# Two causal key tiles scored together, a bias add moved to VectorE, and new weights for the planner of a two-layer gated attention kernel

## The chip, the core and the metric

The kernel runs on one core of one Trainium2 chip. The core has TensorE (PE, matrix products), VectorE (DVE), ScalarE (ACT), GpSimd (POOL) and SyncE (SP, which here only issues transfers); each takes its instructions in order, and semaphores let one wait for another. The metric is the device time of one execution in microseconds. Before the change it is 2710.31 us, the median of three runs (2707.89 to 2714.53).

## What is computed

Eight sequences of 512 tokens and 256 channels pass through two layers. In each layer a gated cross attention and a gated feed-forward part are added to x. Cut to what matters here, with layer 0's attention in full:

```python
# layer 0, attention: 16 heads of 16 channels
q, k, v = heads(x @ Wq + bq), heads(x @ Wk + bk), heads(x @ Wv + bv)
att = q @ k.T * scale
att = where(causal, att, -inf)            # lower triangle of 512 x 512
y = softmax(att) @ v
qc, kc, vc = heads(x @ Wcq + bcq), heads(ctx @ Wck + bck), heads(ctx @ Wcv + bcv)
y = y + softmax(qc @ kc.T * scale) @ vc   # all 512 context rows
xattn = y @ Wp + bp
...
x = x + tanh(g_xattn[0]) * xattn(layernorm(x))
x = x + tanh(g_ffn[0]) * ffn0(layernorm(x))      # 8-bit quantized, gelu
x = x + tanh(g_xattn[1]) * block1(layernorm(x))  # two attention blocks (16 heads of 32), each with an MLP
x = x + tanh(g_ffn[1]) * ffn1(layernorm(x))      # ternary weights, depthwise convolution
```

Everything is float32 except the two feed-forward products, which are bfloat16 after quantization.

## The kernel before

The program is straight-line code that a Python program writes. It has four stages in time: attention of layer 0 (`layer0_xattn`), the first half of layer 0's feed-forward (`layer0_ffn`), then everything else woven together (`layer1_xattn`), with a tail for the last sequence. Between stages x and the hidden values are kept in DRAM.

**Attention of layer 0.** A sequence b is cut into two halves u of the heads, each into two groups e of four heads, and each group has two sides s: s = 0 is causal self attention, s = 1 is attention to the context. A side has four key tiles kt of 128 keys. `steps0` makes the list of steps. `front(e, s, kt)` (L1517) writes four products S = K·Q, one head on each of four 32-row strips of the array, into two PSUM tiles `ps_s` of two banks each; for the causal side only the queries from `lo = 128*kt` on are computed, so tiles 0 to 3 have 512, 384, 256 and 128 columns. Two ACT instructions (L1526) take the exponential from PSUM to `pt`, and for the causal side a GpSimd `affine_select` (L1529) sets the upper triangle of the 128x128 diagonal block of all four heads to zero in place. `back` (L1536) then multiplies with the values, one head on each of four 32-column strips of the array, and accumulates the four key tiles in one PSUM bank `ov` (the value tile holds ones beside the values, so that the sums come with it). After the last key tile DVE transposes `ov` (L1551), takes the reciprocal and scales.

The list holds front, back, front, back, ..., but `end_rest` (L1215) runs the back of the front before: on PE the order is front 1, back 0, front 2, back 1. `ps_s` has three buffers, of which a front takes two; `pt` has two; `ov` has one.

**The other streams.** Around those steps the Python program weaves what else is to be done: `norm0` (layer norm of the next sequence, and L1406, which adds the gated projection bias `gbp` to x once), `pre0` and `values0` (transposes and values), `pairs0` (Q and K of a group), `cross0`, `ctx0`, `post0` (projection and residual), `few_bits` (quantization of weights), `load1`.

**Who sets the order.** `weave_timed` (L1160) and, for the last stage, `weave_all` write one instruction group after another. Each stream has a place on a scale, its base plus its share times the part of it already written; the candidate with the lowest place is written next, among those whose inputs will be there within `soon` of the time at which PE comes free by a table of estimated costs (`Pace`). The numbers that set shares and bases are in `SET`, `FIRST_AT` and `LAST_AT` (L29 to L66, which hold a few others too). `FIRST_AT` and `LAST_AT` place the second half of layer 0's feed-forward (`first`) and layer 1's feed-forward (`last`) of each sequence between the sixteen attention slots of layer 1, in each of which one block of one sequence goes through 4 groups of 4 key tiles. A manual dependency keeps the instructions of every engine in the written order, so the numbers decide what stands behind what on each engine.

In layer 1, `ov` has a single buffer too: after the last key tile of a group the sums come from products with ones ("ps<-acc,ones" and "ps<-pt,ones"), then DVE makes `oT` in four instructions (L2362 to L2367), and only then may the next group's first back write `ov`.

Of the kernel before, what the change touches and what calls it, by code (L numbers as in the profile page):

```python
# [10 lines left out]
AF = mybir.ActivationFunctionType  # L11
ALU = mybir.AluOpType
# [3 lines left out]
P = 128  # L16
B, T, C, CC = 8, 512, 256, 128
H = 16
NT = T // P
# [6 lines left out]
MAGIC = 12582912.0  # L26
NEG = -1.0e30
ROWS = ((0, 1), (2, 3, 4), (5, 6, 7))
FIRST_AT = (-1.51, 0, 1, 2, 4, 3.86, 6.93, 9)  # L29
LAST_AT = (6.01, 6.53, 7.45, 11.96, 12.03, 13, 15)  # L30
PTS = 3
SET = dict(
    pairs0=0.758,
    post0=0.88,
    values0=1.2,
    few0=0.88,
    load1=0.88,
    norm0=0.88,
    ctx0=0.88,
    next0=0.847,  # L40
    gains=0.886,
    range_total=5.807,
    range_share=1.0,
    soon=0.336,
    change0=0.0,
    change1=0,
    first=1.046,
    first_lag=2.213,
    last=0.8,
    last_total=10.064,  # L50
    last_lag=1.534,
    mlp0=0.47,
    mlp1=0.597,
    mlp0_at=1.0,
    mlp1_at=1.0,
    pre=0.65,
    pre_at=-1.433,
    pre_lag=1.558,
    pair=0.2,
    pair_at=-0.25,  # L60
    keys=1.0,
    keys_at=-1.001,
    back=1.05,
    tail_at=17.0,
    half_at=0.0,
# [973 lines left out]
class Fast(General):  # L1039
# [348 lines left out]
    def norm0(self, b):  # L1388
        nc, work, x = self.nc, self.work, self.xs[b]
        if b:  # L1390
            self.load_ctx0(b)
        if 0 < b < B - 1:
            self.load_x0(b + 1)
        q = self.seqs[b]
        z = q["z"] = work.tile([P, NT, C], F32, tag="z", name="z", bufs=1)
        q["recs"] = work.tile([P, 8, 16], F32, tag="recs", name="recs")
        yield need(x, pe=False)
        yield from self.ln_timed(x, z, "n")
        if not b:
# [6 lines left out]
        nc.gpsimd.tensor_tensor(x, x, self.gbp.unsqueeze(1).to_broadcast([P, NT, C]), ALU.add)  # L1406

    def out_of(self, out, ps, scale, bias):

# [93 lines left out]
    def steps0(self, b, u):  # L1503

        nc, work, pace = self.nc, self.work, self.pace
        q = self.seqs[b]
        st = {}

        def front_at(e, s):
            if (u, s) not in q:
                return 1e9
            QT, KT = q[u, s]
            return max(pace.when([Pace.name(QT), Pace.name(KT[e])]), pace.place("st", 2))

        def front(e, s, kt):  # L1517
            QT, KT = q[u, s]
            lo = kt * P if s == 0 else 0
            pss = [self.st.tile([P, 2, T], F32, tag="st", name="ps_s") for _ in range(2)][::-1]  # L1520
            for j in (2, 3, 0, 1):
                r = slice(32 * j, 32 * j + 32)
                self.mm(pss[j // 2][:, j % 2, lo:], KT[e][r, kt * P : (kt + 1) * P], QT[r, lo:])
            pt = work.tile([P, 4, T], F32, tag="pt", name="pt", bufs=2)
            for jp in (1, 0):
                nc.scalar.activation(pt[:, 2 * jp : 2 * jp + 2, lo:], pss[jp][:, :, lo:], AF.Exp)  # L1526
            if s == 0:
                diag = pt[:, :, kt * P : (kt + 1) * P]
                nc.gpsimd.affine_select(  # L1529
                    out=diag, in_=diag, compare_op=ALU.is_ge, fill=0.0,  # L1530
                    base=0, pattern=[[0, 4], [1, P]], channel_multiplier=-1,
                )
            reads = [Pace.name(pt), Pace.name(self.vts[s][b % 2])]
            self.coming = (reads, kt == 0, lambda: back(e, s, kt, lo, pt), lambda: ("v", s) in q)

        def back(e, s, kt, lo, pt):  # L1536
            g = 2 * u + e
            if kt == 0:
# [3 lines left out]
            for j in (2, 3, 0, 1):  # L1542
                self.mm(
                    ov[32 * j : 32 * j + 32, lo:], vt[:, kt, 4 * g + j, :], pt[:, j, lo:],
                    kt == 0, kt == NT - 1,
                )
            if kt < NT - 1:
                return

            ot = work.tile([P, 16, 32], F32, tag="ot", name="ot", bufs=2)  # L1550
            nc.vector.transpose(ot.rearrange("p b d -> p (b d)"), ov)  # L1551
            rec = q["recs"][:, 4 * u + 2 * e + s, :]
            nc.vector.reciprocal(rec, ot[:, :, 16])
            recb = rec.unsqueeze(2).to_broadcast([P, 16, 16])
            if e == 0 and s == 0:
                st["yn"] = work.tile([P, 16, 32], F32, tag="yn", name="yn", bufs=2)
            yn = st["yn"][:, :, 16 * e : 16 * e + 16]
            if s == 0:
                nc.vector.tensor_tensor(yn, ot[:, :, 0:16], recb, ALU.mult)
                return  # L1560
            yc = work.tile([P, 16, 16], F32, tag="yc", name="yc", bufs=2)
            nc.vector.tensor_tensor(yc, ot[:, :, 0:16], recb, ALU.mult)
            nc.vector.tensor_tensor(yn, yn, yc, ALU.add)
            if e == 1:
                yT = self.out0.tile([P, T], F32, tag="yT", name="yT", bufs=3)
                nc.vector.transpose(yT, st["yn"].rearrange("p b d -> p (b d)"))
                q["yT", u] = yT
                if u == 1:
                    self.seen(q["recs"])

        def rest_at():
# [290 lines left out]
    def layer1_xattn(self):  # L1862
        nc, tc = self.nc, self.tc
        with (
# [838 lines left out]
```

## Time and profile before

The profiled execution took 2705.0 us, of which 2703.2 us lie between its first and its last instruction. The stages below are stretches of that span.

| stretch, us | what | PE busy | DVE busy | ACT busy | POOL busy | PE clock |
|---|---|---|---|---|---|---|
| 15 to 100 | layer 0 attention, sequence 0 | 75.6 of 85 | 29.0 | 45.5 | 16.2 | 1.00 |
| 185 to 270 | the same, one sequence later on | 83.4 of 85 | 41.4 | 59.7 | 16.6 | 1.00 |
| 725 to 848 | layer 0 feed-forward, first half | 89.3 of 123 | 95.3 | 81.1 | 1.7 | 0.86 |
| 860 to 2500 | layer 1, woven | 1528.8 of 1640 | 1145.3 | 847.9 | 457.9 | 0.97 |
| 2500 to 2600 | layer 1, last sequences | 84.6 of 100 | 70.8 | 43.3 | 9.4 | 0.95 |
| 2600 to 2704 | tail | 58.0 of 104 | 73.8 | 23.9 | 2.5 | 0.77 |

How to read it: "busy" is the time in which an engine had an instruction at work. For PE an end is modelled, and a product that waits inside its group can be counted as busy, so 98% is not yet PE at its peak. The clock is the share of full speed that the throttle granted to PE in the stretch.

Of the costs that the change touches, the trace has these rows: the exponential takes 1022, 809, 597 and 380 ns for 1024, 768, 512 and 256 elements (L1526), the `affine_select` of L1529 646 ns in the mean (128 of them), and L1406 2362 ns on GpSimd (eight of them).

### The profile page before, as it was taken

The numbers are of one execution on the slowest core, as the hardware profiler recorded it, in microseconds if no ns is written. First come the engines' busy times: TensorE is split into PE (matmuls) and PEld (weight loads), VectorE is DVE, ScalarE is ACT, GpSimd is POOL, SyncE is SP. The second block draws the span as 40 slices with busy tenths as digits, with TensorE's granted clock in tenths as the row PEclk, the third lists the DMA queues.
The fourth block names the chain that finished last, engine by engine and source line by source line (L and its number), as shares of the span: only waits on it lengthen the run. The fifth ranks groups of instructions, "written<-read, shape, count | busy, mean of one in ns | idle before, by whom it ended". The sixth has DMA issues, their size and how long they took to land.

```text
span 2703.2 us, 67872 instructions
## 1 busy us (share of the span) xinstructions
PE 2443.5 (90%) x30128; PEld 1012.8 (37%) x30128; DVE 1711.0 (63%) x3116; ACT 1470.0 (54%) x1831; POOL 614.6 (23%) x682
## 2 busy tenths in 40 slices
PE   6999999999776989999999899999899999999865
PEld 2333333333233334434534433434344444343343
DVE  4444554344377666664576677768856677877767
ACT  4667776666573545544455454455454454655431
POOL 2212222111101444330254221102123431201100
PEclk9999999999987999999999899999999999999987
DMA  3011120100265412210221012021030101201000
GB/s 113 8 48 52 52 74 7 32 33 13 94 281 195 169 48 95 76 63 29 98 69 38 19 45 85 34 87 64 17 122 22 42 28 60 75 29 40 25 25 18
DMA packets 74431, 170.58 MB, mean 63 GB/s; under 512 B 7184, under 2 KB 36240, under 8 KB 66832
## 3 DMA queue, kind: packets, MB, share of 16 engines
q1 hardware_dynamic: 71744, 162.94, 17.2%
q8 instruction: 238, 3.90, 0.6%
q0 software_dynamic: 800, 2.62, 0.3%
q10 hardware_dynamic: 1584, 0.58, 0.1%
q14 instruction: 65, 0.53, 0.1%
HBM read 103.21 MB, written 62.91 MB: 61 GB/s over the span
## 4 chain that ended last, share of the span: by engine, by line


## 5 line engine op out<-in xcount | busy, mean ns | idle before, releaser
L2318 ACT ACTIVATE pt<-ps_s 128x1024 f32<-128x1024 f32 x512 | 496.4, 1021 | 397.0 <-PE ps_s L1146 274.0
L1146 PE MATMUL ps_s<-QT,KT 32*128 32x512 f32 (+3 forms) x4096 | 620.5, 607 | 21.3 <-ACT pt L2318 13.6
L1526 ACT ACTIVATE pt<-ps_s 128x1024 f32<-128x1024 f32 (+3 forms) x512 | 412.2, 862 | 176.9 <-PE ps_s L1146 167.0
L1146 PEld LDWEIGHTS ps_s<-QT,KT 32*128 32x128 f32 x4096 | 194.5, 184 | 381.4 <-issue 189.4
L1146 PE MATMUL ov<-pt,vt 128*32 128x512 f32 (+3 forms) x1792 | 202.0, 521 | 53.2 <-DVE oT L2367 28.5
L1142 PE MATMUL ps<-x3T,li 128*32 128x256 f32 x4096 | 242.1, 389 | 0.1
L1146 PE MATMUL ov<-pt,v 128*32 128x512 f32 (+3 forms) x2048 | 231.1, 521 | 10.5 <-POOL pt L1529 10.5
L1142 PE MATMUL ps<-li,hD 128*32 128x256 f32 x4096 | 231.4, 380 | 5.5 <-ACT hD L2265 5.5
L2322 POOL TENSOR_SCALAR_AFFINE_SELECT dg<-pt 128x512 f32<-128x512 f32 x128 | 121.5, 949 | 477.9 <-ACT pt L2318 477.9
L2078 POOL TENSOR_SCALAR mv<-mv 128x2 f32<-128x2 f32 (+1 forms) x105 | 46.9, 446 | 603.2 <-DVE mv L2073 578.3
L1529 POOL TENSOR_SCALAR_AFFINE_SELECT pt<-pt 128x512 f32<-128x512 f32 x128 | 82.7, 646 | 438.5 <-ACT pt L1526 434.8
L1142 PEld LDWEIGHTS ps<-li,hD 128*32 128x32 f32 x4096 | 133.0, 110 | 98.4 <-issue 11.1
L1142 PEld LDWEIGHTS ps<-x3T,li 128*32 128x32 f32 x4096 | 131.0, 113 | 103.3 <-issue 24.0
L2349 DVE TENSOR_TENSOR acc<-acc,pt 128x2048 f32<-128x2048 f32 x64 | 153.0, 2390 | 2.2 <-ACT pt L2318 0.9
L2347 DVE TENSOR_TENSOR acc<-pt 128x2048 f32<-128x2048 f32 x64 | 151.7, 2370 | 0.0
L2433 DVE SCALAR_TENSOR_TENSOR hF<-hp,cols,hF 128x256 f32<-128x256 f32 x224 | 112.8, 503 | 42.2 <-ACT hF L2424 36.2
L1142 PE MATMUL ps<-zT,a_wq 128*32 128x512 f32 x1024 | 123.5, 602 | 3.6 <-DVE zT L2159 2.3
L1551 DVE STREAM_TRANSPOSE ot<-ov 128x512 f32<-128x512 f32 x64 | 45.8, 715 | 127.8 <-PE ov L1146 127.5
L1142 PE MATMUL ps<-li,oT 128*32 128x256 f32 x2048 | 122.7, 380 | 2.4 <-DVE oT L2367 1.2
L1854 ACT ACTIVATE hD<-ps,cols 128x256 f32<-128x256 f32 x119 | 53.2, 473 | 119.7 <-PE ps L1142 76.7
L1856 DVE TENSOR_SCALAR hD<-ps,cols 128x256 f32<-128x256 f32 x137 | 62.7, 480 | 68.3 <-PE ps L1142 48.1
L2424 ACT ACTIVATE hF<-hp,cols 128x256 f32<-128x256 f32 x54 | 32.4, 600 | 131.8 <-DVE hp L2421 131.8
(304 smaller groups left out, 3578.2 us busy)
## 6 DMA issues: line engine op xcount, KB each, us to landing
hd<-h SPq DMA_DIRECT2D x16, 1024.0 KB, 3.9
hF<-hd SPq DMA_DIRECT2D x16, 1024.0 KB, 6.5
li<-in_w_a_dram SPq DMA_DIRECT2D x12, 1024.0 KB, 5.3
xF<-xd SPq DMA_DIRECT2D x22, 512.0 KB, 5.0
kd<-k SPq DMA_DIRECT2D x8, 1024.0 KB, 5.2
vd<-v SPq DMA_DIRECT2D x8, 1024.0 KB, 5.4
res<-rd SPq DMA_DIRECT2D x32, 256.0 KB, 2.7
vt<-vd SPq DMA_DIRECT2D x8, 1024.0 KB, 5.2
```

Source lines behind the costliest of these rows:

```text
L1142: self.nc.tensor.matmul(out[j : j + 32], lhsT[:, j : j + 32], rhs, start=start, stop=stop, skip_group_check=True)
L1146: self.nc.tensor.matmul(out, lhsT, rhs, start=start, stop=stop, skip_group_check=True)
L1526: nc.scalar.activation(pt[:, 2 * jp : 2 * jp + 2, lo:], pss[jp][:, :, lo:], AF.Exp)
L1529: nc.gpsimd.affine_select(out=diag, in_=diag, compare_op=ALU.is_ge, fill=0.0, base=0, pattern=[[0, 4], [1, P]], channel_multiplier=-1,)
L1854: self.nc.scalar.activation(out, ps, AF.Identity, bias=bias)
L1856: self.nc.vector.tensor_scalar(out, ps, bias, None, ALU.add)
L2078: nc.gpsimd.tensor_scalar(rstd, mv[:, :, 1], EPS, None, ALU.add)
L2318: nc.scalar.activation(pt[:, 2 * jp : 2 * jp + 2, :], pss[jp], AF.Exp)
L2322: nc.gpsimd.affine_select(out=dg, in_=pt[:, :, diag], compare_op=ALU.is_gt, fill=0.0, base=0, pattern=[[0, 4], [-1, P]], channel_multiplier=1,
L2347: nc.vector.tensor_tensor(st["acc"], st["pt"], pt, ALU.add)
L2349: nc.vector.tensor_tensor(st["acc"], st["acc"], pt, ALU.add)
L2433: nc.vector.scalar_tensor_tensor(a, hp[:, half + k : half + k + n], self.col("conv_w", 3 * f + k), a, ALU.mult, ALU.add)
```

## The change

Three edits. (1) `front` and `back` take a list of key tiles. On the causal side the four steps (0), (1), (2), (3) become three, (0), (1, 3), (2): the 128 columns of tile 3 and the 384 of tile 1 stand side by side in the same two `ps_s` tiles (tile 3 at columns 0 to 127, tile 1 behind), one pair of exponentials takes all 512, and one `affine_select` takes both diagonal blocks, which stand at columns 0 to 255. The back multiplies tile 1, then tile 3, into `ov`; key tile 2 is now the last. The context side keeps its four steps. (2) L1406 is issued on VectorE instead of GpSimd. (3) Some 25 numbers of the planner are set anew, which rewrites the order of all stages.

The number of PE products and the columns that they run over stay as they were. Counted in the two written programs, layer 0's attention has 255 runs of row-strip products before and 223 after; 256 and 224 runs of column-strip products; 26 and 26 of whole-array transposes. In layer 1 the same counts are 256 and 256, 282 and 286, 86 and 85.

```diff
-FIRST_AT = (-1.51, 0, 1, 2, 4, 3.86, 6.93, 9)
-LAST_AT = (6.01, 6.53, 7.45, 11.96, 12.03, 13, 15)
+FIRST_AT = (-1.51, -0.4, 1, 2, 4, 3.86, 7.6, 9)
+LAST_AT = (6.01, 6.53, 8.78, 11.96, 12.49, 13, 16.76)
 SET = dict(
-    pairs0=0.758,
-    post0=0.88,
-    values0=1.2,
+    pairs0=1.659,
+    post0=0.932,
+    values0=0.0,
...
-    norm0=0.88,
-    ctx0=0.88,
-    next0=0.847,
-    gains=0.886,
+    norm0=0.541,
+    ctx0=1.787,
+    next0=0.959,
+    gains=1.202,
...
-    soon=0.336,
+    soon=0.475,
...
-    pre=0.65,
+    pre=1.019,
...
-    pair_at=-0.25,
-    keys=1.0,
-    keys_at=-1.001,
+    pair_at=-0.48,
+    keys=0.91,
+    keys_at=-0.936,
...
-        nc.gpsimd.tensor_tensor(x, x, self.gbp.unsqueeze(1).to_broadcast([P, NT, C]), ALU.add)
+        nc.vector.tensor_tensor(x, x, self.gbp.unsqueeze(1).to_broadcast([P, NT, C]), ALU.add)
...
-        def front(e, s, kt):
+        def front(e, s, kts):
             QT, KT = q[u, s]
-            lo = kt * P if s == 0 else 0
+            at, parts = 0, []
+            for kt in kts[::-1]:
+                lo = kt * P if s == 0 else 0
+                parts.insert(0, (kt, lo, slice(at, at + T - lo)))
+                at += T - lo
             pss = [self.st.tile([P, 2, T], F32, tag="st", name="ps_s") for _ in range(2)][::-1]
-            for j in (2, 3, 0, 1):
-                r = slice(32 * j, 32 * j + 32)
-                self.mm(pss[j // 2][:, j % 2, lo:], KT[e][r, kt * P : (kt + 1) * P], QT[r, lo:])
+            for kt, lo, cols in parts:
+                for j in (2, 3, 0, 1):
+                    r = slice(32 * j, 32 * j + 32)
+                    self.mm(pss[j // 2][:, j % 2, cols], KT[e][r, kt * P : (kt + 1) * P], QT[r, lo:])
             pt = work.tile([P, 4, T], F32, tag="pt", name="pt", bufs=2)
             for jp in (1, 0):
-                nc.scalar.activation(pt[:, 2 * jp : 2 * jp + 2, lo:], pss[jp][:, :, lo:], AF.Exp)
+                nc.scalar.activation(pt[:, 2 * jp : 2 * jp + 2, :at], pss[jp][:, :, :at], AF.Exp)
             if s == 0:
-                diag = pt[:, :, kt * P : (kt + 1) * P]
+                diag = pt[:, :, : len(kts) * P]
                 nc.gpsimd.affine_select(
                     out=diag, in_=diag, compare_op=ALU.is_ge, fill=0.0,
-                    base=0, pattern=[[0, 4], [1, P]], channel_multiplier=-1,
+                    base=0, pattern=[[0, 4], [0, len(kts)], [1, P]], channel_multiplier=-1,
                 )
...
+            end = (2, 3)[s]
+            for kt, lo, cols in parts:
+                for j in (2, 3, 0, 1):
+                    self.mm(
+                        ov[32 * j : 32 * j + 32, lo:], vt[:, kt, 4 * g + j, :], pt[:, j, cols], kt == 0, kt == end
+                    )
+            if parts[-1][0] != end:
                 return
...
-                for kt in range(NT):
-                    ops.append((lambda e=e, s=s: front_at(e, s), lambda e=e, s=s, kt=kt: front(e, s, kt), "rows"))
+                for kts in ((0,), (1, 3), (2,)) if s == 0 else ((0,), (1,), (2,), (3,)):
+                    ops.append((lambda e=e, s=s: front_at(e, s), lambda e=e, s=s, kts=kts: front(e, s, kts), "rows"))
```

The names after the change keep their meaning; the line of the exponential moves from L1526 to L1531, that of the select from L1529 to L1534, and that of the bias add stays L1406.

More of the change, by code (lines that the diff above doesn't have):

```diff
@@ L28 @@
 ROWS = ((0, 1), (2, 3, 4), (5, 6, 7))
-FIRST_AT = (-1.51, 0, 1, 2, 4, 3.86, 6.93, 9)
-LAST_AT = (6.01, 6.53, 7.45, 11.96, 12.03, 13, 15)
+FIRST_AT = (-1.51, -0.4, 1, 2, 4, 3.86, 7.6, 9)
+LAST_AT = (6.01, 6.53, 8.78, 11.96, 12.49, 13, 16.76)
 PTS = 3
 SET = dict(
-    pairs0=0.758,
-    post0=0.88,
-    values0=1.2,
-    few0=0.88,
-    load1=0.88,
-    norm0=0.88,
-    ctx0=0.88,
-    next0=0.847,
-    gains=0.886,
+    pairs0=1.659,
+    post0=0.932,
+    values0=0.0,
+    few0=0.936,
+    load1=0.886,
+    norm0=0.541,
+    ctx0=1.787,
+    next0=0.959,
+    gains=1.202,
     range_total=5.807,
     range_share=1.0,
-    soon=0.336,
-    change0=0.0,
-    change1=0,
+    soon=0.475,
+    change0=0,
+    change1=0.0013,
     first=1.046,
-    first_lag=2.213,
-    last=0.8,
+    first_lag=1.838,
+    last=0.736,
     last_total=10.064,
     last_lag=1.534,
-    mlp0=0.47,
+    mlp0=0.49,
     mlp1=0.597,
     mlp0_at=1.0,
-    mlp1_at=1.0,
-    pre=0.65,
-    pre_at=-1.433,
-    pre_lag=1.558,
+    mlp1_at=0.987,
+    pre=1.019,
+    pre_at=-1.436,
+    pre_lag=1.538,
     pair=0.2,
-    pair_at=-0.25,
-    keys=1.0,
-    keys_at=-1.001,
+    pair_at=-0.48,
+    keys=0.91,
+    keys_at=-0.936,
     back=1.05,
@@ L1515, in front_at, with back @@
             return max(pace.when([Pace.name(QT), Pace.name(KT[e])]), pace.place("st", 2))
-        def front(e, s, kt):
+        def front(e, s, kts):
             QT, KT = q[u, s]
-            lo = kt * P if s == 0 else 0
+            at, parts = 0, []
[3 more added lines that the diff above has]
+                at += T - lo
             pss = [self.st.tile([P, 2, T], F32, tag="st", name="ps_s") for _ in range(2)][::-1]
-            for j in (2, 3, 0, 1):
-                r = slice(32 * j, 32 * j + 32)
-                self.mm(pss[j // 2][:, j % 2, lo:], KT[e][r, kt * P : (kt + 1) * P], QT[r, lo:])
+            for kt, lo, cols in parts:
+                for j in (2, 3, 0, 1):
+                    r = slice(32 * j, 32 * j + 32)
+                    self.mm(pss[j // 2][:, j % 2, cols], KT[e][r, kt * P : (kt + 1) * P], QT[r, lo:])
             pt = work.tile([P, 4, T], F32, tag="pt", name="pt", bufs=2)
             for jp in (1, 0):
-                nc.scalar.activation(pt[:, 2 * jp : 2 * jp + 2, lo:], pss[jp][:, :, lo:], AF.Exp)
+                nc.scalar.activation(pt[:, 2 * jp : 2 * jp + 2, :at], pss[jp][:, :, :at], AF.Exp)
             if s == 0:
-                diag = pt[:, :, kt * P : (kt + 1) * P]
+                diag = pt[:, :, : len(kts) * P]
                 nc.gpsimd.affine_select(
                     out=diag, in_=diag, compare_op=ALU.is_ge, fill=0.0,
-                    base=0, pattern=[[0, 4], [1, P]], channel_multiplier=-1,
+                    base=0, pattern=[[0, 4], [0, len(kts)], [1, P]], channel_multiplier=-1,
                 )
             reads = [Pace.name(pt), Pace.name(self.vts[s][b % 2])]
-            self.coming = (reads, kt == 0, lambda: back(e, s, kt, lo, pt), lambda: ("v", s) in q)
-        def back(e, s, kt, lo, pt):
+            self.coming = (reads, kts[0] == 0, lambda: back(e, s, parts, pt), lambda: ("v", s) in q)
+        def back(e, s, parts, pt):
             g = 2 * u + e
-            if kt == 0:
+            if parts[0][0] == 0:
                 st["ov"] = self.ovp.tile([P, T], F32, tag="ov", name="ov")
@@ L1541, in back @@
             vt = q["v", s]
[L1542 to L1547, printed above, removed]
+            end = (2, 3)[s]
[5 more added lines that the diff above has]
+            if parts[-1][0] != end:
                 return
```

## The prediction

> **What bounds the kernel now.** I read the busy times first, then the slices, then windows by stage.
>
> ```profile
> PE 2443.5 (90%) x30128; PEld 1012.8 (37%) x30128; DVE 1711.0 (63%) x3116; ACT 1470.0 (54%) x1831; POOL 614.6 (23%) x682
> ...
> PE   6999999999776989999999899999899999999865
> ...
> PEclk9999999999987999999999899999999999999987
> ```
>
> PE carries the span; slices 2 to 10 (layer 0's attention, about 15 to 707 us) are full at full clock, so there every microsecond less of PE work or stall is a microsecond less of span. In layer 1 PE is 1528.8 of 1640 us busy, with small stalls everywhere. The last 165 us depend on DVE; no score product is left there, and the two written programs differ little in it, so I book nothing for it.
>
> Busy time hides stalls inside a group of products. The PE timeline shows them by the distance from start to start:
>
> ```profile
> 147.97 0.93 PE L1146 MATMUL ps_s<-QT,KT 32*128 32x384 f32 x8
> 148.83 1.07 PE L1146 MATMUL ov<-pt,v 128*32 128x512 f32 x8
> 149.82 1.20 PE L1146 MATMUL ps_s<-QT,KT 32*128 32x256 f32 x8
> 151.73 0.85 PE L1146 MATMUL ov<-pt,v 128*32 128x384 f32 x8 [0.70 <-POOL pt L1529]
> 152.51 0.50 PE L1146 MATMUL ps_s<-QT,KT 32*128 32x128 f32 x8
> 152.94 0.64 PE L1146 MATMUL ov<-pt,v 128*32 128x256 f32 x8
> 153.51 1.16 PE L1146 MATMUL ps_s<-QT,KT 32*128 32x512 f32 x8
> 154.60 0.43 PE L1146 MATMUL ov<-pt,v 128*32 128x128 f32 x8
> 154.96 1.99 PE L1146 MATMUL ps_s<-QT,KT 32*128 32x512 f32 x8
> 156.88 1.06 PE L1146 MATMUL ov<-pt,v 128*32 128x512 f32 x8
> ```
>
> Scores of 384 columns take 0.86 us to the next start and those of 128 take 0.43, so 128 columns cost 0.215 and a turn from scores to values 0.215 more. The backs give 0.99, 0.78, 0.57 and 0.36 for 512 to 128 columns: 0.21 per 128 and about 0.145 for the turn back. At these prices the 256-column front (149.82) should take 0.645 and took 1.91: a stall of 1.27, since its successor waited for the select of tile 1. The second context front (154.96) should take 1.07 and took 1.92: 0.85, waiting for a score buffer that ACT was still reading. The same subtraction over 26 to 707 us leaves 67 us, 50 of them after fronts (28 after 512 columns, 14 after 256, 4 each after 384 and 128) and 6 after backs: 56 in the attention steps.
>
> **1. The merge, turns.** The written order has 32 runs of scores and 32 of values fewer (255 to 223, 256 to 224): 32 x (0.215 + 0.145) = **-11.5 us**. Columns and products are the same. PE is full there, so all of it counts.
>
> **2. The merge, ACT and POOL.** Two exponential pairs of 809 and 380 ns become one of 1022: 2 x 167 ns x 32 = 10.7 us less on ACT, which is 59.7 of 85 us busy. That isn't span by itself; it shortens the waits of step 3. Two selects of 637 ns become one of twice the elements, which the trace doesn't show: from 0.64 (all fixed) to 1.27 us (all by element). The Trainium skill (GPSIMD Engine Reference, section 3.1) puts the best loop at about 1.8 cycles per element at 1.2 GHz, which for 1024 elements would be 1.54 us and for 512 would be 0.77, while the row has 0.637. By the rule the merged tile comes 0.27 us later than by the row's upper end, 32 x 0.27 = 8.6 us if nothing covers it. The row decides; I take 1.2, near the upper end.
>
> **3. Stalls in layer 0.** A back needs its exponentials (2.04 us a pair of 512 columns), its select and about 0.25 of signals after its front; between them PE has one back, one front and what is woven in. The merged tile needs 2.04 + 1.2 + 0.25 = 3.5 us and has 0.215 + 0.99 + 0.645 = 1.85: alone it is 1.65 short, so it must be filled by another stream (a projection of 16 products lasts 1.7). Tile 2 behind it has a merged back and a 512 front, 2.1 us, against 1.19 + 0.64 + 0.25: none short. I counted both orders with these prices. Before, backs come too early by 28.6 us in sum and fronts find the score buffer taken for 12.9: 41.5, where the trace has 56. After, the sums are 8.8 and 3.0: the new weights put the fillers where the merged tile needs them (something stands behind the merged front in 23 of 32 places and behind the 256 front in 22; before, behind the 384 front in 14 and the 256 front in 22). Scaled by 56/41.5 the 11.8 become 16, a gain of 40 at most. The count doesn't see KT evacuations that stand between exponentials on ACT (1.45 us for two at 148.12), and one stall covers the next. Ends: 0 and -40; nearer to the count than to nothing, I take **-25**.
>
> **4. The bias add on DVE.** Eight adds of 2362 ns leave POOL. What they cost now:
>
> ```profile
> 127.35 2.36 POOL L1406 TENSOR_TENSOR x<-x,gbp 128x1024 f32<-128x1024 f32 x1
> 129.67 0.64 POOL L1529 TENSOR_SCALAR_AFFINE_SELECT pt<-pt 128x512 f32<-128x512 f32 x1
> ...
> 128.54 1.20 DVE L2082 SCALAR_TENSOR_TENSOR mv<-mv 128x4 f32<-128x4 f32 x1
> ```
>
> The select runs directly behind the add, and a DVE instruction of 128x4 elements, 0.17 us elsewhere (10.91), lasts until the add ends. On DVE the nearest rows are two-input adds of 2048 elements, 2283 ns in the median, and 128x1024 (L2460) at 1283: 1.2 us each, 9.6 in all, in a stage where DVE is half idle (41.4 of 85). Seven are covered; uncovered they would cost 8.4. Against this edit speaks the Trainium skill (SBUF — State Buffer, section "SBUF: two separate sides"): VectorE with two SBUF inputs and a GpSimd operation that reads SBUF share an exclusive lock, and the later one waits for the whole instruction. The 1.20 us above agrees. So each add can hold a select for up to 1.2 us: 8.4 by the rule if all meet one on the path. By the rows the same lock held 1.03 us of DVE and the add itself the select: I book **0** for the seven. Queued behind the add on DVE in the written order are scale factors of the weights, the context's normalization and the residual; PE waits for those only through a transpose.
>
> The first add is uncovered. In the opening DVE makes `gbp` and then copies the second half of xnT at 17.85, for which PE waits; the new order puts the add between them: **+1.2 us**.
>
> **5. The new weights in layer 1.** No work is added: turns nearly balance (282 and 286 value runs, 256 score runs, 86 and 85 transposes), 2 us at most. What moves is distance. A group ends with sums; then DVE makes oT (0.71 + 0.25 + 0.71 + 0.69 us) before the next back may write the single `ov`.
>
> ```profile
> PE ov L1146 <- DVE oT L2367: 28.5, 20, 3.0
> PE ov L1146 <- DVE mv L2082: 21.0, 7, 5.7
> PE ps_s L1146 <- ACT pt L2318: 13.6, 20, 2.9
> ```
>
> With 2.7 us needed, 20 of 63 group ends have too little PE work between in the order before, 20.8 us short in sum; the trace has exactly 20 waits for oT. In the new order it is 29 of 63, 34.0 short. Fronts that find the score buffers taken go from 29.7 to 37.5; the waits from the last products of ffn1 to its row maximum +2; from sums to the output projection -2.5. The nominal sum is +20. `soon` from 0.336 to 0.475 lets the planner accept such waits in return for an order it prefers, and a stall that is paid once gives DVE and ACT time to catch up, so they don't add. From 0 to +41 (the 49.5 us of waits for DVE scaled by 34.0/20.8, +31, with the buffers' 8 and 2): I take half the nominal, **+10**.
>
> **Sum:** -11.5 - 25 + 0 + 1.2 + 10 = -25 against the profiled 2705.0, or 2680. The median of the runs shown lies 5.3 above the profiled execution: **2685 us**. A measurement tells about 0.3%, 8 us, from no change.
>
> **The rivals.**
> A. Everything pays: the stalls go as counted (-40) and layer 1 keeps its time: -11.5 - 40 + 1.2 = -50, **2660**. For it: the count matched the 20 oT waits. Against: it ignores ACT's other work.
> B. The stalls in layer 0 only move: the merged tile waits 1.65 us where the 384 and 256 ones waited; the turns alone are gained, and layer 1 takes its +10 or nothing: between -10 and 0, **2704**. For it: ACT and the select are later in one piece; 9 merged fronts have no filler directly behind.
> C. DVE becomes the bound at the group ends of layer 1: +41 as above, with -20 from layer 0 (turns and a third of the stalls) and the opening's 1: +22, **2732**. DVE is 70% busy in layer 1, and DVE work per group exceeds PE work by 17 us in sum before and 34 after, by the same prices. It decides once those losses pass layer 0's 35: when the 29 short ends cost (49.5 + 35)/29 = 2.9 us each, against 1.8 now (49.5 in 27).
> That the change doesn't do what it says is excluded by the 32 runs of each kind that are gone from the written program.
>
> **Chances.** Forecast 0.48 (its own range 2672 to 2700), A 0.20, B 0.17, C 0.15. Faster by over 0.3%: forecast, A and half of B, 0.76. Within: the other half of B, 0.09. Slower: C, 0.15. The range leaves out the upper part of C and the last of A: 2655 to 2718.
>
> **What would show it.** Turns: 32 runs fewer, and start-to-start of a merged front near 1.07 where ACT is early. ACT: 384 exponentials of 1024 elements at 1022 ns in layer 0. Select: a row of 128x1024, 32 of them, between 0.64 and 1.27. Layer 0's last back should end near 672 instead of 707. Step 4: no 1.2 us L2082; xnT copied 1.2 us later in the opening. Step 5: waits for oT and `mv` L2082 together near 60 rather than 49.5. I am wrong in step 3 if PE's waits for the merged select pass 16 us, and in the sign if layer 1's last front moves by more than layer 0 gained.

## The result, and the profile after

The change makes the kernel 10 us faster: a median of 2701.2 us (seven runs, 2699.5 to 2704.2) against 2711.4 us (seven runs, 2705.0 to 2714.5), a ratio of 0.9965 with a 95% interval of 0.9954 to 0.9977. The prediction said 25 us. The profiled execution of after took 2701.9 us with a span of 2700.0; the one of before happened to be the fastest of its seven (2705.0), so the two traces differ by only 3.2 us of span.

The page of after, busy times and slices:

```profile
PE 2441.2 (90%) x30128; PEld 1023.6 (38%) x30128; DVE 1720.4 (64%) x3137; ACT 1458.0 (54%) x1761; POOL 577.9 (21%) x642
...
PE   6999999999676898999999989999999989999876
...
PEclk9999999999887999999999999999999999999987
```

PE is still the bound, and slices 2 to 10 are as full as before. "Full" hides the difference; start-to-start distances show it. I cut each trace at two points: the start of the first score product, and the start of the last group of value products of layer 0.

| | opening, to the first score | layer 0's attention | rest of the span |
|---|---|---|---|
| before | 26.8 | 674.8 | 2001.6 |
| after | 28.2 | 657.0 | 2014.9 |
| difference | +1.3 | **-17.8** | +13.3 |
| predicted | +1.2 | **-36.5** | +10 |

The middle column is where the prediction failed. The subtraction used in the prediction (start to start, less the price of columns and turn), applied to layer 0 of both traces, splits it. The turns give their 11.5 us. The stalls of the attention steps go from 56 to 47, where 25 us less were expected. The other streams, and what fits no price, take 2.4 us back. By place, in us:

| stall after | before | after |
|---|---|---|
| the first two fronts of all, which have no back between them | 1.7 | 1.7 |
| causal fronts: tile 0; tiles 1 and 3; tile 2 | 1.7; 7.4; 13.8 | 7.0; 2.4; 7.3 |
| context fronts: 1st, 2nd, 3rd, 4th | 8.7, 8.6, 3.0, 4.2 | 1.1, 1.4, **20.5**, 0.5 |
| backs | 6.8 | 5.2 |
| other streams, above the shortest distance that the same group shows in any run here | 1.8 | 3.0 |

What the merge was meant to shorten did get shorter, and so did three of the four context fronts. But 17.5 us came up in one new place, the third context front: 1.17 us in 15 of its 32 occurrences and 0.23 in 13 others. Another 5.3 us came up at the first causal front. Here is a third context front, in the timeline of after (start, duration, engine, line, operation, tile, shape, count; in brackets the engine's idle time before it and what ended it):

```profile
149.49 1.14 PE L1146 MATMUL ps_s<-QT,KT 32*128 32x512 f32 x8
...
150.72 1.94 ACT L1531 ACTIVATE pt<-ps_s 128x1024 f32<-128x1024 f32 x2 [0.99 <-PE ps_s L1146]
...
151.06 1.04 PE L1142 MATMUL ps<-ctxT,wck_p 128*32 128x512 f32 x8
151.31 0.72 DVE L1557 STREAM_TRANSPOSE ot<-ov 128x512 f32<-128x512 f32 x1 [3.43 <-PE ov L1146]
...
152.03 1.14 PE L1146 MATMUL ps_s<-QT,KT 32*128 32x512 f32 x8
152.06 0.25 DVE L1559 RECIPROCAL recs<-ot 128x16 f32<-128x16 f32 x1
...
152.69 0.80 DVE L1414 TENSOR_SCALAR KT<-ps,par,kbe 128x512 f32<-128x512 f32 x1
...
153.52 0.78 ACT L1412 ACTIVATE KT<-ps,kbe,par 128x512 f32<-128x512 f32 x1 [0.86 <-DVE KT L1414]
...
154.09 2.30 PE L1146 MATMUL ps_s<-QT,KT 32*128 32x512 f32 x8
154.20 3.76 ACT L1531 ACTIVATE pt<-ps_s 128x1024 f32<-128x1024 f32 x4
...
156.32 1.07 PE L1146 MATMUL ov<-pt,v 128*32 128x512 f32 x8
```

Read it from the end. The third context front (154.09) takes 2.23 us to the next start where its price is 1.07: it has to wait for a score buffer, which is free only when ACT has read it. ACT starts those exponentials at 154.20, because the copy of a key half (L1412) stands before them, and that copy starts at 153.52 after 0.86 us of waiting for DVE. The K product of `pairs0` (151.06) leaves its sums in one PSUM bank, from which `out_of` copies two halves, one for each group e. The planner gave the first half to DVE and the second to ACT, and the program orders them. The product was through at about 152.1, but DVE first had a transpose, a reciprocal and a scaling to do and reached its half at 152.69. ACT was free at 152.66 and stood still behind a queue that wasn't its own, and all exponentials behind it came 0.86 us later.

The waits before L1412 in the whole trace (us, times) put a number on that. Of after, the first two lines:

```profile
  DVE KT L1414: 32.6, 25
  PE ps L1142: 10.3, 7
```

Before, the wait for DVE was 22.3 us in 17 places.

The other rows that answer the prediction, from the groups by shape of after (busy us, mean ns, idle time before):

```profile
L1531 ACT ACTIVATE pt<-ps_s 128x1024 f32<-128x1024 f32 x384 | 369.3, 1023 | 156.0 <-PE ps_s L1146 149.7 <-PE ov L1146 3.5
...
L1534 POOL TENSOR_SCALAR_AFFINE_SELECT pt<-pt 128x1024 f32<-128x1024 f32 x32 | 35.5, 1108 | 66.9 <-ACT pt L1531 66.9
...
L1406 DVE TENSOR_TENSOR x<-x,gbp 128x1024 f32<-128x1024 f32 x8 | 12.9, 1618 | 0.1
```

The 384 long exponentials are there at 1023 ns; the merged select takes 1.11 us, between the ends of 0.64 and 1.27 and near the 1.2 taken; the add takes 1.62 us in the mean on DVE, 1.19 at its shortest.

In layer 1 the waits of PE from 850 us to the end (us in total, times, longest) are, after:

```profile
PE ov L1146 <- DVE oT L2373: 37.3, 25, 4.5
PE ps_s L1146 <- ACT pt L2324: 22.6, 28, 4.1
PE ov L1146 <- DVE mv L2088: 17.0, 8, 3.5
```

The sum of the two waits for DVE went from 49.5 to 54.3, and the waits for score buffers from 13.6 to 22.6.

### The profile page after: what moved, and what is told of

It is laid out like the page before. It is cut to its first block, busy times and chain, and to the rows that moved or that the text cites. A ratio compares the mean times of both kernels' runs of the same rounds, so it can differ in the third digit from the quotient of the medians.

```text
span 2700.0 us, 67756 instructions
## 1 busy us (share of the span) xinstructions
PE 2441.2 (90%) x30128; PEld 1023.6 (38%) x30128; DVE 1720.4 (64%) x3137; ACT 1458.0 (54%) x1761; POOL 577.9 (21%) x642
## 4 chain that ended last, share of the span: by engine, by line
PE 46%; DVE 14%; ACT 4%; issue 2%; POOL 2%; ACTq 0%; POOLq 0%; DVEq 0%
PE ps L1142 28%; PE ps_s L1146 8%; PE ov L1146 5%; PE ps L1146 3%; ACT pt L2324 2%; DVE acc L2353 1%; DVE hF L2439 1%; PE ps L1149 1%; DVE mv L2078 1%; DVE rb L2371 1%; DVE rt L2368 1%; DVE oT L2373 1%; POOL dg L2328 1%; DVE hm L2449 1%; POOL res L2150 1%
## 5 line engine op out<-in xcount | busy, mean ns | idle before, releaser
L1146 PE MATMUL ps_s<-QT,KT 32*128 32x512 f32 (+3 forms) x4096 | 619.7, 604 | 27.0 <-ACT pt L2324 22.6
L1531 ACT ACTIVATE pt<-ps_s 128x1024 f32<-128x1024 f32 (+1 forms) x448 | 403.3, 962 | 173.8 <-PE ps_s L1146 167.2
L1146 PE MATMUL ov<-pt,v 128*32 128x512 f32 (+3 forms) x2048 | 224.7, 520 | 5.5 <-POOL pt L1534 5.5
L1534 POOL TENSOR_SCALAR_AFFINE_SELECT pt<-pt 128x512 f32<-128x512 f32 (+1 forms) x96 | 79.4, 831 | 427.8 <-ACT pt L1531 427.8
L2085 POOL TENSOR_TENSOR mv<-mv,mhalf 128x2 f32<-128x2 f32 (+1 forms) x121 | 103.7, 857 | 10.1
```

What stands on the lines that cost most here:

```text
L1146: self.nc.tensor.matmul(out, lhsT, rhs, start=start, stop=stop, skip_group_check=True)
L1531: nc.scalar.activation(pt[:, 2 * jp : 2 * jp + 2, :at], pss[jp][:, :, :at], AF.Exp)
L1534: nc.gpsimd.affine_select(out=diag, in_=diag, compare_op=ALU.is_ge, fill=0.0, base=0, pattern=[[0, 4], [0, len(kts)], [1, P]], channel_mul ...
L2085: nc.gpsimd.tensor_tensor(rstd, rstd, self.mhalf[:, :nt], ALU.pow)
```

## The experiments

My theory after the result was: the merge and the numbers save what was counted, but ACT's wait for DVE's key half eats most of it. The rivals were those on record (the stalls only move because the merged tile is late; layer 1 or DVE takes the gain back) and, for the edits that I had booked at nothing, that they had cost or brought something. The table gives all twelve kernels. The ratio of each is to the runs of before that were taken beside it, whose median lay between 2711.2 and 2713.7; the last two columns come from the profiled execution of each, by the cuts used above.

| run | what | median us | ratio to before, 95% | layer 0 | rest |
|---|---|---|---|---|---|
| before | | 2711.4 | | 674.8 | 2001.6 |
| after | | 2701.2 | 0.9965 (0.9954 to 0.9977) | 657.0 | 2014.9 |
| e1 | after, both key halves on one engine | 2683.9 | 0.991 (0.9887 to 0.9933) | 637.9 | 2014.1 |
| e2 | after, add on GpSimd | 2707.5 | 0.999 (0.9978 to 1.0003) | 663.1 | 2016.6 |
| e3 | after, layer 1's numbers of before | 2692.9 | 0.9945 (0.9928 to 0.9961) | 655.0 | 2005.0 |
| e4 | after, layer 0's numbers of before | 2729.2 | 1.0067 (1.0045 to 1.0089) | 682.2 | 2017.2 |
| e5 | after, key halves exchanged | 2682.3 | 0.99 (0.988 to 0.992) | 640.0 | 2007.6 |
| e6 | e1 with e3 | 2684.7 | 0.9892 (0.9871 to 0.9913) | 638.3 | 2020.5 |
| e7 | before, both key halves on one engine | 2706.3 | 0.9985 (0.9974 to 0.9996) | 675.7 | 2006.9 |
| e8 | before, merge alone | 2734.7 | 1.009 (1.0072 to 1.0108) | 698.1 | 2009.7 |
| e9 | before, numbers alone | 2733.5 | 1.0081 (1.0067 to 1.0094) | 680.0 | 2018.5 |
| e10 | e5 with e3 | 2681.7 | 0.9885 (0.9866 to 0.9905) | 637.9 | 2007.7 |

In e1, e2, e5, e6, e7 and e10 the planner goes on counting the moved instruction on the engine where it stood, so that the written order stays that of the kernel it is derived from; only the engine differs. e3 keeps the order of layer 0, e4 (but for a few groups) that of layer 1, as in after.

### e1: both halves of a key pair on one engine

```diff
-    def out_of(self, out, ps, scale, bias):
+    def out_of(self, out, ps, scale, bias, on=None):
...
-        if self.pace.sooner(0.2 + 0.001 * n, 0.16 + 0.0011 * n):
+        plan = "Activation" if self.pace.sooner(0.2 + 0.001 * n, 0.16 + 0.0011 * n) else "DVE"
+        self.pace.planned = plan
+        if (on or plan) == "Activation":
...
+        self.pace.planned = None
+        return on or plan
...
+            on = None
             for e in range(2):
-                self.out_of(KT[e], ps, self.par[:, e : e + 1], self.kbe[:, s, u, e : e + 1])
+                on = self.out_of(KT[e], ps, self.par[:, e : e + 1], self.kbe[:, s, u, e : e + 1], on)
```

> The changed kernel in its own written order; only the second half of each K pair (KT, layer 0) goes to the engine that evacuates the first half, so ScalarE never waits for VectorE's half of the same PSUM bank. Theory: the exponentials behind that wait are what holds the score buffers; the 13 stalls of 1.16 us after the third context front and the 7 of 0.67 us after the first causal front go, layer 0's last back starts 15 to 20 us earlier (near 670 instead of 687.5), time 2682 to 2687, ratio to before 0.989 to 0.991. Rival (ScalarE's 2.04 us a step against TensorE's 2.07 is itself the bound): last back near 687, time 2699 to 2704.

Layer 0 takes 637.9 us: 19.1 less than after, and 36.9 less than before. About 1.7 of the 19.1 are not the edit's: after has a stretch of low clock from 46 to 50 us (0.57 in the mean), where e1 has 1.00. The stalls of the attention steps fall from 47.1 to 29.1 us, those after the third context front from 20.5 to 6.5, and no wait of the key copy on ACT for DVE is left. But the edit also takes 23 more of these copies from ACT than it brings there, 23 x 0.777 = 18 us of work, so it doesn't yet tell "the order of two readers" from "less work on ACT". e5 does.

### e5: the same work on each engine, the other one first

In the 25 pairs that after splits with DVE first, ACT now takes the first half and DVE the second; both engines keep the same kinds of copies, at the same places in their queues.

```diff
             for e in range(2):
-                self.out_of(KT[e], ps, self.par[:, e : e + 1], self.kbe[:, s, u, e : e + 1])
+                on = ("Activation", "DVE")[e] if swap else None
+                self.out_of(KT[e], ps, self.par[:, e : e + 1], self.kbe[:, s, u, e : e + 1], on)
```

> The changed kernel with, in the 25 pairs of key halves of layer 0 whose first half is on DVE and second on ACT, the two engines exchanged: ACT takes the first half, DVE the second. Every engine has the same instructions in the same order. Theory (ACT's half waits in front of the exponentials until a DVE that is behind has read the same PSUM bank): ACT no longer waits for DVE, the waits of the KT activation for DVE fall from 32.6 us to under 4, third context fronts lose most of their 22 us of stalls, time near 2686 (2680 to 2692). Rival 1 (with both halves on DVE it was the 18 us less work on ACT that paid): ACT's work is as before, time stays near 2700. Rival 2 (the wait only changes sides): DVE now waits for ACT and its copies for the next projections come later; time 2695 or more.

2682.3 us, as fast as e1, with ACT's work as in after (1460.1 us busy, against 1458.0). In layer 0 e5 takes 640.0 us, 17.0 less than after. So it is the order that costs, some 17 us of layer 0, and not the amount of work on ACT. What the key copy on ACT waits for, in e5:

```profile
  PE ps L1145: 18.0, 15
  PE ps_s L1145: 9.1, 2
...
  DVE KT L1419: 67.7, 27
```

The first two lines are its own waits: only for the product. The last is what waits for it: DVE, 67.7 us in 27 places, more than twice what ACT had waited before, and it costs nothing that shows: e5 gains as much as e1. My reading, which no run tests by itself, is that what is queued behind it on DVE is not awaited so soon, and that the second half is for the later group. The same spot in the PE timeline of e5:

```profile
150.15 1.14 PE L1149 MATMUL ps_s<-QT,KT 32*128 32x512 f32 x8
151.22 1.07 PE L1149 MATMUL ov<-pt,v 128*32 128x512 f32 x8
152.22 1.37 PE L1149 MATMUL ps_s<-QT,KT 32*128 32x512 f32 x8
153.52 1.06 PE L1149 MATMUL ov<-pt,v 128*32 128x512 f32 x8
```

The third context front (152.22) takes 1.30 us to the next start instead of 2.23. That the two copies may not simply run side by side is what the Trainium skill states (PSUM — Partial Sum Buffer, section "PSUM bank collisions raise a hardware error": two engines must not be at the same bank and partitions at once, two readers included). No run here tries it without the order; the runs show what the wrong order costs at this place: 14.0 of the 20.5 us are gone in e5.

### e7: the same edit on the kernel before

> The kernel before, with both halves of a key pair on one engine and nothing else. There ACT waits for DVE's half 22.3 us in 17 places, where the changed kernel has 32.6 in 25, and its second and third context fronts stall 8.1 and 8.4 us. Theory (the wait costs the fronts of either kernel): 2711 - 17 x 22.3/32.6 = 2699. Rival (it is the change that put the wait on the path; before, the fronts waited for the select or the buffers anyway): 2708 or more.

Layer 0 takes 675.7 us against 674.8, but that hides a gain. PE has the same order in both, so that the traces can be compared product by product: until 46 us e7 falls 4.5 us behind, with a clock of 0.68 between 30 and 46 us where before has 1.00, and from there to the end of layer 0 it gains 3.5 us. The median is 5 to 6 us lower, at the edge of what can be told (the interval ends at 0.9996). So the result lies between the theory (2699) and the rival (2708 or more), nearer to the rival: of the 22.3 us of waiting on ACT that were there before, only some 3.5 were on the path. That the merge and the new numbers made the other waits shorter, and put the K product next to the context fronts, where a late ACT is felt, is how I read the difference; no run moves the K product alone.

### e4, e8, e9: merge and numbers, together and apart

e4 is after with the old numbers for the streams of layer 0; e8 and e9 are before with one of the two edits, and with the add on GpSimd.

```diff
 SET = dict(
-    pairs0=1.659,
-    post0=0.932,
-    values0=0.0,
+    pairs0=0.758,
+    post0=0.88,
+    values0=1.2,
...
-    norm0=0.541,
-    ctx0=1.787,
-    next0=0.959,
-    gains=1.202,
+    norm0=0.88,
+    ctx0=0.88,
+    next0=0.847,
+    gains=0.886,
...
-            can = [c for c in cands if c[1] <= now + SET["soon"]]
+            can = [c for c in cands if c[1] <= now + SET["soon0"]]
```

That is e4, with `soon0` at 0.336 for layer 0 and 0.475 kept for layer 1. e8 takes from the change's diff only `front`, `back` and the list of steps, e9 only `FIRST_AT`, `LAST_AT` and `SET`.

> The changed kernel, but with layer 0's weights of before; layer 1's order is that of the changed kernel. Theory (turns are gained by the merge alone, 11.5 us, and the new weights only shift stalls from the 256-column and context fronts to the third context front): time within 4 us of the changed kernel, 2697 to 2706. Rival (the merged tile needs the new weights, which put a filler behind it): last back 8 to 20 us later than 687.5, time 2709 to 2720.

> The kernel before with the merged front of key tiles 1 and 3 alone: all numbers of the planner as before, the add on GpSimd. The prediction's reading (32 turns fewer are a gain wherever the fillers stand, and stalls do not grow): 2711 - 11.5 = 2700 or less. The rival reading (the merged tile needs 3.5 us and has 1.85 unless another stream stands behind it, and the old numbers do not put one there): slower than before, 2720 to 2732, with layer 0's last value product after 707 us.

> The kernel before with the new numbers of the planner alone: four fronts as before, the add on GpSimd. Theory (the numbers are worth something only with the merge, since the fillers that they move stand where the merged tile needs them, and their cost in layer 1 stays): layer 0 within 10 us of before and +4 to +8 in layer 1, 2708 to 2722. Rival (the numbers are what made the kernel faster, and the merge brought little): 2701 or less.

With the add on GpSimd, layer 0 takes, in us:

| | four fronts | merged front |
|---|---|---|
| numbers of before | 674.8, clock 1.00 (before) | 698.1, clock 0.97 (e8) |
| numbers of after | 680.0, clock 1.00 (e9) | 663.1, clock 0.99 (e2) |

Each edit alone makes the kernel slower: e8 by 22 us and e9 by 20, against the runs of before beside them, and both (2734.7 and 2733.5), like e4 (2729.2), are slower than theory and rival had said. Only together do they gain. The PE timeline of e8 shows where the merge alone stalls:

```profile
160.32 1.15 PE L1146 MATMUL ps_s<-QT,KT 32*128 32x384 f32 x16
161.40 1.06 PE L1146 MATMUL ov<-pt,v 128*32 128x512 f32 x8
162.39 1.19 PE L1146 MATMUL ps_s<-QT,KT 32*128 32x256 f32 x8
164.96 1.07 PE L1146 MATMUL ov<-pt,v 128*32 128x384 f32 x16 [1.38 <-POOL pt L1534]
```

Nothing stands between the merged front and its back but one back and one front. The front at 162.39 takes 2.57 us to the next start at a price of 0.645: a stall of 1.93, against the 1.65 that the prediction worked out for a merged tile without a filler. In after, the same place reads:

```profile
144.06 1.15 PE L1146 MATMUL ps_s<-QT,KT 32*128 32x384 f32 x16
145.13 1.92 PE L1142 MATMUL ps<-xnT,wcq_p 128*32 128x512 f32 x16
146.88 1.04 PE L1146 MATMUL ov<-pt,v 128*32 128x512 f32 x8
147.85 0.71 PE L1146 MATMUL ps_s<-QT,KT 32*128 32x256 f32 x8
148.49 1.07 PE L1146 MATMUL ov<-pt,v 128*32 128x384 f32 x16
```

A projection (145.13) fills the gap, and the 256-column front takes its price. e4 and e8 both lose 24 us after the fronts of tile 2, against 7.3 in after.

This stall isn't all of e8's loss. Over its layer 0 the granted clock was 0.968, against 1.000 in before; if PE could have used all of that clock, the loss is up to 22 us (an estimate: 3.2% of 698), and without it layer 0 would take about 676 us, as in before. So the stalls eat the 11.5 us of the turns, and the rest of e8's 23 us in layer 0 may be clock. PE also waits 11.8 us in four places for key halves from DVE (2.4 us in before), as here, where a DVE addition, 0.43 us in the median, lasts 2.48 while the bias add runs on GpSimd:

```profile
311.15 2.52 POOL L1406 TENSOR_TENSOR x<-x,gbp 128x1024 f32<-128x1024 f32 x1
311.48 2.48 DVE L1569 TENSOR_TENSOR yn<-yn,yc 128x256 f32<-128x256 f32 x1
...
315.50 1.53 DVE L1414 TENSOR_SCALAR KT<-ps,par,kbe 128x512 f32<-128x512 f32 x2
...
317.18 2.65 PE L1142 MATMUL ps<-wp_p,yT 128*32 128x256 f32 x32 [3.77 <-DVE KT L1414]
```

The shares of these causes, and whether the waits bring the low clock, no run separates. Of e9 the trace gives the parts: layer 0 +5.2 and the rest +16.9 us against before. The latter is more than the numbers cost in layer 1 in e3; the planner also wrote the rest in another order than in after, and what costs the time there is not settled.

### e2: the add back on GpSimd

```diff
+        self.pace.planned = "DVE"
-        nc.vector.tensor_tensor(x, x, self.gbp.unsqueeze(1).to_broadcast([P, NT, C]), ALU.add)
+        nc.gpsimd.tensor_tensor(x, x, self.gbp.unsqueeze(1).to_broadcast([P, NT, C]), ALU.add)
+        self.pace.planned = None
```

> The changed kernel in its own written order, with only the bias add back on GpSimd. Theory (the add on VectorE is covered, on GpSimd it holds selects): opening 1.2 us earlier, the seven other adds cost 0 to 1 us each, time 2700 to 2706, ratio 0.996 to 0.998. Rival (the lock that VectorE's two-input add takes is what costs layer 0): last back earlier by 4 to 8 us, time 2693 to 2697.

6.3 us slower than after in the medians (just beyond the 2706 expected), and 6.1 in layer 0. The edit that I had booked at nothing is worth more than half of what the whole change gained. The opening did not get shorter as expected: the copy of xnT follows `gbp` at once, but `gbp` itself came 1.3 us later in this execution.

PE has the same order in both kernels, so the two traces show where e2 falls behind. 3.6 us come at one place, the second add. In e2:

```profile
39.19 3.54 DVE L179 TENSOR_SCALAR ctx<-ctx,mv 128x128 f32<-128x128 f32 x4 [2.85 <-POOL mv L2090]
40.31 2.34 POOL L1410 TENSOR_TENSOR x<-x,gbp 128x1024 f32<-128x1024 f32 x1
42.65 0.68 DVE L1440 TENSOR_TENSOR v<-ps,rows 128x512 f32<-128x512 f32 x1
43.38 3.47 PE L1145 MATMUL ps<-xnT,wcq_p 128*32 128x512 f32 x16 [3.58 <-DVE v L1440]
```

and the same place of after:

```profile
39.23 1.47 DVE L179 TENSOR_SCALAR ctx<-ctx,mv 128x128 f32<-128x128 f32 x4 [2.85 <-POOL mv L2085]
40.62 0.68 DVE L1435 TENSOR_TENSOR v<-ps,rows 128x512 f32<-128x512 f32 x1
41.22 1.21 DVE L1406 TENSOR_TENSOR x<-x,gbp 128x1024 f32<-128x1024 f32 x1
41.36 1.92 PE L1142 MATMUL ps<-xnT,wcq_p 128*32 128x512 f32 x16 [1.51 <-DVE v L1435]
```

While the add runs on GpSimd, the last of DVE's four scalings of the context is held until it ends; the values come 2 us later, and PE waits 3.58 us for them instead of 1.51. The projection behind that wait then takes 3.47 us instead of 1.92: from 42 to 46 us e2 was granted a clock of 0.64, and after 1.00. So about 1.5 of the 3.6 us are clock.

Most of the rest, 1.9 us, comes in four steps of 0.4 to 0.6 us at the next four adds, where a back waits 0.2 us for a select that had to stand behind the add. Two more steps of 0.3 and 0.4 us have no add beside them. In after it is the add on DVE that is stretched by a GpSimd select, from 1.2 to as much as 2.0 us, and no instruction in the trace waits for it.

### e3, e6, e10: layer 1's old numbers

```diff
-FIRST_AT = (-1.51, -0.4, 1, 2, 4, 3.86, 7.6, 9)
-LAST_AT = (6.01, 6.53, 8.78, 11.96, 12.49, 13, 16.76)
+FIRST_AT = (-1.51, 0, 1, 2, 4, 3.86, 6.93, 9)
+LAST_AT = (6.01, 6.53, 7.45, 11.96, 12.03, 13, 15)
...
-    pre=1.019,
+    pre=0.65,
...
-    pair_at=-0.48,
-    keys=0.91,
-    keys_at=-0.936,
+    pair_at=-0.25,
+    keys=1.0,
+    keys_at=-1.001,
...
-            can = [c for c in cands if c[1] <= now + SET["soon"]]
+            can = [c for c in cands if c[1] <= now + SET["soon1"]]
```

The last lines are those of layer 1, with `soon1` at 0.336.

> The changed kernel, but with layer 1's weights of before (FIRST_AT, LAST_AT and those of the last stage, soon too); layer 0's order is that of the changed kernel. Theory of the prediction (the new layer 1 order costs about 10 us): layer 0 ends at 687.5, time 2690 to 2695, ratio 0.992 to 0.994. Rival 1 (the new weights of layer 1 are neutral or gain): 2700 to 2708. Rival 2 (start of layer 1 alone lost): the first group of layer 1 ends 14 to 18 us earlier than in before, and the gain stays from there.

8 us faster than after, by the medians; the median clock was 0.965, against 0.963. PE's waits in layer 1 go back to where they were (20 for oT):

```profile
PE ov L1147 <- DVE oT L2374: 30.4, 20, 3.0
PE ov L1147 <- DVE mv L2089: 21.0, 7, 5.7
PE ps_s L1147 <- ACT pt L2325: 14.8, 20, 2.9
```

So the new numbers of layer 1 cost something near what step 5 had booked, and they are not needed for the gain in layer 0. How much is open: the rest of the span took 2001.6 to 2020.5 us in the six kernels with the old numbers there (median 2007.3), and 2007.6 to 2017.2 in the five with the new ones in the order of after (median 2014.9). Then the fix and the old numbers together:

> The changed kernel with both halves of a key pair on one engine and with layer 1's numbers of before. If the two gains stand in different stages and add up (2701.2 to 2683.9 by the first, to 2692.9 by the second), 2675.6, ratio near 0.987. If layer 1 takes a fixed time from its last due times whatever layer 0 gained, near 2684.

> The changed kernel with the 25 split key pairs exchanged (ACT takes the first half) and layer 1's numbers of before; the edit of e5 and that of e3 together. At equal granted clock the edit of e3 was worth 4 us and that of e5 14 to 16: 2682.3 - 4 = 2678, ratio near 0.988. If the two overlap, 2682 to 2685, as the run with both halves on one engine and layer 1's old numbers gave (2684.7).

2684.7 and 2681.7 us: by the medians, nothing on top of e1 and e5, and the intervals of all four lie on each other. One reason can be read in the runs: the granted clock. In the six runs of e1 the time goes from 2678.5 us at a clock of 0.966 to 2691.3 at 0.960, in the five of e6 from 2676.5 at 0.965 to 2690.5 at 0.958: 2 us for each 0.001. The median clock was 0.964 in e1 and 0.960 in e6. At 0.963, by that slope, e1 would have 2685 and e6 2680; but levelling by a clock is a calculation, and the runs as measured don't separate them. All four beat both kernels, by 27 to 32 us on the runs of before beside them.

## Why the prediction was off

- **Step 1, turns, -11.5: right.** The runs of products are gone, and a merged front takes 1.07 us to the next start (144.06 to 145.13 in after).
- **Step 2: right.** The merged select takes 1.11 us (1.2 taken); the 1.54 us that I had estimated from the Trainium skill's 1.8 cycles per element (GPSIMD Engine Reference, section 3.1) does not hold for this select, and the row that I had preferred to it does.
- **Step 3, stalls, -25: this is the step that failed; measured, about -9 in the attention steps.** The count of buffers and fillers was sound: with the key halves out of the way (e1) the stalls of those steps fall from 56 to 29 us, 27 less where I had said 25. (That layer 0 as a whole then comes out 36.9 us shorter than before, against my 36.5, is in part luck, since it includes the add, which e2 puts at 6 and step 4 at nothing.) What failed is how I treated the gap in the count. I wrote that it doesn't see the key copies between exponentials on ACT, and allowed for that by taking 25 of 40. But I looked only at their duration (1.45 us for two) and not at what they wait for: ACT's half waits for DVE's half, and DVE's queue holds a transpose, a reciprocal and a scaling. In after that wait is 32.6 us in 25 places, and removing it by order alone (e5) gives 17 us back. The trace of before had it too, 22.3 us in 17 places; I never asked the ACT lines what ended their idle time. My warning sign (16 us of PE waits for the merged select) was put at the wrong place: those waits are 3.9 us in after, and the loss shows as stalls inside score groups.
- **Step 4, add, 0 and +1.2: the opening was right in its mechanism, the seven others mis-sized; 0 should have been about -6, of which some 1.5 are clock** (e2). In the opening of after the add (18.54) stands in front of the copy of xnT (19.68), and PE waits 1.56 us for it, where it waits 0.23 in e2. The whole opening is no measure of that: with one and the same order it took 28.2 us in after and 29.8 in e3. For the rest I set the lock's loss on DVE off against the same lock afterwards, and didn't ask which of the two waiting instructions somebody waits for.
- **Step 5, +10: right in sign, and not contradicted in size:** 8 us in the medians (e3), some 4 of which the slope of 2 us for each 0.001 of clock would explain; 13 in the two profiles of before and after; oT and mv waits 54.3 us where I had said near 60, buffers +9.0 where the count had +8.
- **The rivals.** B (2704) came nearest in time, and its sentence "the stalls in layer 0 only move" is what happened; but not by its mechanism. The merged tile is not late in after. It is late without the new numbers (e4, e8), where the stalls eat the gain. C didn't happen: the 25 waits for oT cost 1.5 us each.

Sum as measured, in the two profiles: opening +1.3, turns -11.5, stalls of the attention steps -8.7, other streams and the unassigned +2.4, rest +13.3: -3.2 us of span. In the medians, 10 us.

## What to carry to other kernels

When two engines copy halves out of one PSUM bank and the program orders them, as here, the second waits for whatever the first engine still has in its queue, so give the first half to the engine whose next work is awaited soonest: here that alone, with no work moved, was worth 17 us in layer 0 (19 in the medians), where the merge of tiles with all its planning had brought 10. A merge that makes a tile later pays only if something is put into the gap, so its numbers belong to it: apart, each half lost some 20 us. When you count stalls from durations and buffers, also read, for every instruction on the critical engine, what ended its idle time: a wait that is harmless now is the next bound once the others are gone.

## What the runs showed of the hardware

- A long wait need not cost anything: DVE waits 67.7 us for ACT in e5, and the kernel is 19 us faster than with ACT waiting 32.6 us for DVE.
- Moving an add between DVE and GpSimd moves who is stretched: a group of four DVE instructions went from 1.47 to 3.54 us beside a GpSimd add, and the add itself, on DVE beside a GpSimd select, from 1.2 to 2.0.
- A change of the written order can change the granted clock: over layer 0 it was 1.000 in before and 0.968 in e8, up to 22 us of 698 by the estimate above, and over the whole span all five runs of e8 had 0.952 to 0.956, where the runs of before beside them had 0.959 to 0.968.
- The granted clock differs between runs of one kernel by up to 0.009, and with it the time by 17 us (before, 2697.9 us at 0.968 and 2714.6 at 0.959), more than the change itself was worth. A single profile against a single profile (3.2 us here) is no measure of a change of 10.
